# One row of steps for both batches' attention, with the first values behind two scores and the last values ahead of their sums

## The chip, the cores and the metric

The kernel runs on one core of a Trainium2 chip. The metric is the device time of one launch in microseconds (us), as a median over several executions. The engines are called as the profile calls them: PE is TensorE (PEld its weight loads), DVE VectorE, ACT ScalarE, POOL GpSimd, SP SyncE, which issues most DMAs.

## What is computed

Two layers on an input `x` of 2 batches x 256 channels x 56 x 56 pixels (3136 tokens a batch), all in fp32. The first is a linear non-local block (three 1x1 convolutions in 8 groups, no softmax), with a residual and a relu. The second is causal attention with 4 heads of 64, and then a mixture of 8 experts with the two best per token. Cut to what matters here:

```
x = relu(conv_block(x) + x)                          # layer 0
t = tokens(x)                                        # (2, 3136, 256)
q, k, v = heads(layernorm(t) @ W_attn)               # 4 heads of 64
att = softmax(where(causal, q @ k.T / 8, -big))
t = t + (att @ v) @ W_proj
g = layernorm(t);  probs = softmax(g @ gate_w + gate_b)
top2_vals, top2_idx = top_k(probs, 2)                # gate values are not renormalised
t = t + sum over the two experts e: w_e * (gelu(g @ W1[e] + b1[e]) @ W2[e] + b2[e])
```

## The kernel before

Names: `b` is the batch (B = 2), `hp` the pair of heads (NH = 2), `i` a block of 448 queries (NB = 7, W = 448), `j` a chunk of 128 keys (NCH = 25, the last has 64). Scores are held with keys on the partitions and two heads x 448 queries along the free axis, 896 elements.

**First layer** (0 to some 80 us): Gram matrices of `x`, folded into one matrix per batch, which is applied to `x`. The tokens `ts[b]` stay on chip and are also written to DRAM as `kept`.

**Attention, the fast path** (80 to some 850 us, batch 0 and then batch 1). For every (b, i, hp) the chunks that the causal mask admits are gone through. A *step* is one chunk: `scores` makes the products (L745, 8 PE instructions), exps without subtracting a maximum (ACT, L753), masks (DVE, L755, only on a chunk that the diagonal cuts) and adds the exps into an accumulator `acc` (DVE: the first chunk is copied, L763, the others added, L767). `values` multiplies the same exps with the values (L785) into a PSUM bank `yp`. Values run LAG = 3 steps behind the scores. When the last values of a (b, i, hp) are done, ACT copies `yp` into the tile that `acc` holds (L796) and POOL adds the two halves into `qT`, over the queries that are no longer needed (L797):

```
both = accs.pop((hp, i))
nc.scalar.copy(both, yp[:, :, :W])
nc.gpsimd.tensor_tensor(yh, both[:, 0], both[:, 1], ALU.add)
```

`sum_rows` makes the denominators: products of `acc` with ones (L809), an ACT copy (L814), and two DMAs by way of DRAM into row r = (b * 2 + hp) * 7 + i of a tile `sums`. The tasks in `later` follow some steps afterwards: `invert` (reciprocal, DMA out, two DMAs back, spread over the partitions), `scale` (L841) and `hand_on`, which tells by `finished` that these queries may be projected.

In every iteration n of the loop over steps, the order that all five engines keep is written out by hand: BEHIND = 2 steps after a (b, i, hp) has issued its last scores come `visit` (projections of the next block's queries, keys and values, L600 to L638) and its `sum_rows`; then `between` (pulls a piece of other work from a queue: projecting back, gate, dispatch, loads), due tasks, scores of step n, values of step n - 3. Where the values are the first of a (b, i, hp), the scores come ahead of them. Every batch has a row of steps and a call of `attend` of its own.

**Experts** (some 850 us to the end): tokens are sorted by expert into blocks of 128 slots. Rows are scattered to DRAM by indirect DMA on POOL (L1420), loaded block by block (102 blocks in the main loop, MAIN), transposed (L1518), multiplied (L1541, gelu on ACT at L1550, L1560) and gathered or added back into tokens (`finish`, gathers at L1738). `meanwhile` pulls queued work once a block; batch 1's scattering lies beside the first blocks.

**The second path.** `judge` looks, after batch 1's denominators, at the least and greatest element of `sums` on each partition; the number of partitions on which both lie in the bounds is kept in `good`, and in another element of it multiplied with whether the blocks were enough:

```
nc.vector.tensor_scalar(tiles[:, 2:3], tiles[:, 0:1], MOST, None, ALU.is_le)    # MOST = 1e25
nc.vector.tensor_scalar(tiles[:, 3:4], tiles[:, 1:2], LEAST, None, ALU.is_ge)   # LEAST = 1e-25
```

At the end of the program stands

```
with tc.If(n_done < P):
    n_good = count(0)
    with tc.If(n_good < P):
        ...                    # reads kept[b] back, statistics of every row
        layer1("g", True)
    late()
```

`layer1("g", True)` is the whole second layer once more, with names that end in `_g`: `attend_general` subtracts the true maximum of every query before the exps. It takes one head and 112 queries at a time, keeps the scores of all chunks in SBUF, has one PSUM bank for scores, one for values, and leaves the order of engines to the scheduler. `late()` is for blocks beyond the main loop and writes the whole output again.

Of the kernel before, what the change touches and what calls it, by code (L numbers as in the profile page):

```python
# [28 lines left out]
def conv_attn_moe_kernel(  # L29
# [482 lines left out]
    def layer1(nm, general):  # L512

        with ExitStack() as whole:
# [192 lines left out]

            def attend(
                b, qT, kT, v, fst, fs, psc, py, visit, between, clock, later, finished
            ):  # L710

                steps, firsts = [], {}
                for i in range(NB):
                    nk = -(-((i + 1) * W) // P)
                    whole_js = [j for j in range(nk) if (j + 1) * P - 1 <= i * W]
                    cut = [j for j in range(nk) if j not in whole_js]

                    order = whole_js[: max(0, len(whole_js) - len(cut))]  # L720
                    rest = whole_js[len(order) :]
                    if not order and rest:
                        order.append(rest.pop(0))
                    while cut or rest:
                        if cut:
                            order.append(cut.pop(0))
                        if rest:
                            order.append(rest.pop(0))
                    for hp in range(NH):
                        for r, j in enumerate(order):  # L730
                            steps.append((i, hp, j, r == 0, r == len(order) - 1, order))
                sts, accs, yps = {}, {}, {}

                def scores(n):
                    i, hp, j, first, last, order = steps[n]
# [25 lines left out]
                    if first:  # L761
                        acc = fs.tile([P, 2, W], F32, tag="acc", name=f"acc_{sn}")
                        nc.vector.tensor_copy(acc, st)  # L763
                        accs[hp, i] = acc
                    else:
                        acc = accs[hp, i]
                        nc.vector.tensor_tensor(  # L767
                            acc[:k, :, c0:], acc[:k, :, c0:], st[:k, :, c0:], ALU.add
                        )
                    sts[n] = st  # L770

                def values(n):
                    i, hp, j, first, last, order = steps[n]
# [4 lines left out]
                    if first:  # L778
                        yps[hp, i] = py.tile([P, 2, 512], F32, tag="y", name=f"yp_{sn}")
                    yp = yps[hp, i]  # L780
# [11 lines left out]
                    if last:  # L792

                        yh = qT[:, hp, i * W : (i + 1) * W]
                        both = accs.pop((hp, i))
                        nc.scalar.copy(both, yp[:, :, :W])  # L796
                        nc.gpsimd.tensor_tensor(yh, both[:, 0], both[:, 1], ALU.add)  # L797
                        del yps[hp, i]

                def sum_rows(hp, i):  # L800
# [3 lines left out]
                    acc = accs[hp, i]  # L804
# [18 lines left out]
                    later.append((clock[0] + 4, invert, hp, i, yh))  # L823

                def invert(hp, i, yh):
# [12 lines left out]
                    later.append((clock[0] + 6, lambda hp, i, yh: scale(hp, i, yh, rb), hp, i, yh))  # L838

                def scale(hp, i, yh, rb):  # L840
                    nc.vector.tensor_tensor(yh, yh, rb, ALU.mult)  # L841
                    later.append((clock[0] + 2, hand_on, hp, i, yh))

                def hand_on(hp, i, yh):
                    finished[hp] = (i + 1) * W

                def due(now):
                    while later and (now is None or later[0][0] <= now):
                        _, task, hp, i, yh = later.pop(0)
                        task(hp, i, yh)  # L850
                        later.sort(key=lambda e: e[0])

                ends = {i: max(n for n, s in enumerate(steps) if s[0] == i) for i in range(NB)}
                LAG, BEHIND = 3, 2
                for n in range(len(steps) + LAG):
                    if BEHIND < n <= len(steps) + BEHIND and steps[n - 1 - BEHIND][4]:
                        i, hp = steps[n - 1 - BEHIND][:2]
                        visit(i, hp)
                        sum_rows(hp, i)
                    if n < len(steps):  # L860
                        i = steps[n][0]
                        between(i, ends[i] - n, (steps[n][2] + 1) * P > i * W + 1)

                    late = n >= LAG and steps[n - LAG][3]
# [7 lines left out]
                    if late:  # L872
                        values(n - LAG)
                return due
# [561 lines left out]
            def experts(w1s, w2s, b2s, ex, es, ps6, between, need, written, settle, decide):  # L1436
# [63 lines left out]
                def experts_of(r):  # L1500

                    b = 0 if (r + 1) * GB <= FULL0 else 1
                    s = r * GB - known[b][0]
                    return nc.values_load_multi_w_load_instructions(
                        eblks[b][0:1, s : s + GB],
                        engines=(PE, DVE),
                        min_val=0,
                        max_val=E - 1,
                        skip_runtime_bounds_check_because="a count of at most E parts, cut to E - 1",
                    )[1]  # L1510

                def inputs(n, group):
                    xb, to = group
                    g = n % GB
# [165 lines left out]
                for n in range(-1, MAIN + 1):  # L1680
# [4 lines left out]
                    if n < 0:  # L1685
                        ids.extend(experts_of(0))
# [5 lines left out]
                    for m in (n + 1, n + 2):  # L1692
                        if m < MAIN and m not in wb:
                            wb[m] = weights(m)
                    if n == MAIN - 1:
                        decide()
# [21 lines left out]

            def finish(b, oy, bufs):
# [3 lines left out]
                def fetch(n, m, k):  # L1723
# [9 lines left out]
                    for c, y in enumerate(ys):  # L1733
                        for a in range(m):
                            while gathered[0] == 1 + turn[0] % 2:
                                yield False
# [61 lines left out]
                ahead, added = deque(), None  # L1798
                parts = deque(pairs())
                if b:  # L1800
                    parts = deque([(0, 1, P), *pairs(1, LAST)])
                while b == 0 and (parts or ahead):
                    if parts:
                        yield from fetch(*parts.popleft())
                    if len(ahead) == bufs or not parts:
# [184 lines left out]
            else:  # L1990
# [9 lines left out]
                def ahead(b, i, hp):  # L2000

                    xs, qks, vs = projections[b]
                    if i + 1 < NS:
                        if hp == 0:
                            return qks(i + 1), xs(i + 2)[:1]
                        return vs(i + 1), xs(i + 2)[1:]
# [3 lines left out]
                    if hp == 0:  # L2010
                        return [], xs(0)
                    return qks(0) + vs(0), xs(1)
# [20 lines left out]
                for piece in keys[2:] + vs(0) + xs(1):  # L2033
                    piece()
                for b in range(B):
                    batches.append(tokens(b, qT, lambda b=b: min(finished[b])))
# [4 lines left out]
                    def visit(i, hp):  # L2041

                        now, then = ahead(b, i, hp)
                        if b + 1 == B and i + 1 == NB and hp + 1 == NH:
                            nc.scalar.activation(warm, eps5[:1], AF.Gelu)
                        ring.append(0)
                        for piece in now:
                            piece()
                        for _ in range(2):
                            products()  # L2050
                        for piece in then:
                            piece()
                        ring.clear()

                    def between(i, left, cut):
                        if b == B - 1 and i == NB - 1 and left < NH * NCH - 2:

                            now = load_w2(left < NCH - 4)
                            for _ in range(1 if left > NCH - 4 else 2):
                                next(now, None)  # L2060

                        tick[0] += 1
                        if not cut or i:
                            pull()

                    due = attend(
                        b, qT, kT, v, fst, fs, psc, py, visit, between,
                        clock, later, finished[b],
                    )
# [20 lines left out]
            with ExitStack() as moe:  # L2090
# [23 lines left out]
                def written():  # L2114
# [4 lines left out]
                    for a in range(GB):  # L2119
                        hots.append(hot.tile([P, REST], F32, name=f"hot{a}_{nm}"))  # L2120
                        nc.gpsimd.iota(
                            hots[a], pattern=[[1, REST]], base=LAST * P - OFF, channel_multiplier=0,
                            allow_small_or_imprecise_dtypes=True,
                        )
# [3 lines left out]
                def meanwhile():  # L2128
                    gathered[0] = stored[0] = 0
                    turn[0] += 1  # L2130
                    if placed[1] and not sent[1]:
                        pull(2 + turn[0] % 2, every=True)
# [4 lines left out]
                    if side and next(side[0], None) is None:  # L2137
                        side.popleft()

# [10 lines left out]
                with tc.manual_schedule(engines={PE, DVE, POOL, SP, ACT}):  # L2150
                    experts(
                        first[0], w2s, b2s, ex, es, ps6,
                        meanwhile, need, written, settle, decide,
# [173 lines left out]
```

## Time and profile before

| | us |
|---|---|
| median of 3 runs (1262.29 to 1263.56) | 1262.87 |
| profiled execution | 1279.51 |
| its span | 1277.8 |
| PE busy in the span | 1251.2 |
| DVE / ACT / POOL busy | 786.6 / 613.2 / 357.9 |
| first layer, window 0 to 80: PE busy | 76.67 |
| attention of batch 0, window 80 to 464: PE busy | 381.63 |
| attention of batch 1, window 464 to 852: PE busy | 382.81 |
| experts, window 852 to 1277.8: PE busy | 410.08 |

The profiled execution is one of its own and 16.6 us longer than the median; durations and waits are read from it. The mean granted PE clock in it is 0.998. A row of the groups reads: line, engine, operation, output<-inputs, shape, count | busy us in total, mean ns of one | idle us of that engine just before, and what ended it. The ends of matmuls are modelled, so that a row's mean on PE times its count overstates the time in which PE works; the windows and the page count overlaps once. Lines are those of the kernel that the row belongs to.

### The profile page before, as it was taken

Reading aid. Unit: us, or ns where it says so; the run is one execution under the profiler, and the core shown is the slowest. Engines: PE = TensorE matmul, PEld = TensorE weight load, DVE = VectorE, ACT = ScalarE, POOL = GpSimd, SP = SyncE. Lnnn points to the kernel's source line nnn. Section 1 sums busy time; section 2 is a strip of 40 time slices with the busy share of each in tenths; the row PEclk is TensorE's granted clock in tenths of the full one; section 3 lists DMA queues with packets and bytes.
Section 4 is the critical chain, followed back from the end, with each engine's and each line's share of the span. In section 5 each row is a group of like instructions: output and inputs, shape, how many; then the busy total and the mean of one; then the engine's idle time right before and its main releaser. Section 6 shows DMA issues by size and latency. Waiting matters only on the chain.

```text
span 1277.8 us, 28550 instructions
## 1 busy us (share of the span) xinstructions
PE 1251.2 (98%) x10809; PEld 816.4 (64%) x10809; DVE 786.6 (62%) x1711; ACT 613.2 (48%) x1237; POOL 357.9 (28%) x319
## 2 busy tenths in 40 slices
PE   8999999999999999999999999999999999999998
PEld 8875545444444444545544443469889899899996
DVE  2673567666777745576677878785744443455664
ACT  0255555565556555455555655553333333344432
POOL 1103230000002204221102666100256112666651
PEclk9999999999999999999999999999999999999999
DMA  9995001000000000100000123541334333466654
GB/s 312 357 346 177 24 18 32 25 9 25 9 17 10 25 1 17 35 16 9 9 9 22 66 71 100 199 137 65 100 130 150 105 113 101 142 198 199 212 160 126
DMA packets 111073, 123.87 MB, mean 97 GB/s; under 512 B 19703, under 2 KB 100840, under 8 KB 110930
## 3 DMA queue, kind: packets, MB, share of 16 engines
q1 hardware_dynamic: 100274, 95.41, 24.2%
q0 software_dynamic: 9840, 25.67, 6.0%
q8 instruction: 89, 1.46, 0.5%
q10 hardware_dynamic: 816, 0.88, 0.2%
q14 instruction: 54, 0.44, 0.1%
HBM read 62.06 MB, written 61.05 MB: 96 GB/s over the span
## 4 chain that ended last, share of the span: by engine, by line
PE 93%; DVE 3%; issue 1%; ACT 1%; another core or an unknown queue 0%; DVEq 0%; DMA 0%; ACTq 0%
PE yp_f L785 20%; PE sc_f L745 20%; PE ht_f L1541 14%; PE yp_f L1560 13%; PE qk_f L614 7%; PE v_f L629 4%; PE pp_f L683 3%; PE cp L410 3%; PE gram L317 2%; PE tp_f L1518 2%; DVE acc_f L767 1%; PE sp_f L809 1%; PE yo_f L1787 1%; PE xp_f L600 1%; ACT st_f L753 1%
## 5 line engine op out<-in xcount | busy, mean ns | idle before, releaser
L767 DVE TENSOR_TENSOR acc_f<-acc_f,st_f 128x896 f32<-128x896 f32 (+5 forms) x372 | 373.1, 1003 | 127.2 <-ACT st_f L753 117.4
L753 ACT ACTIVATE st_f<-sc_f 128x896 f32<-128x896 f32 (+5 forms) x400 | 330.4, 838 | 203.2 <-PE sc_f L745 182.8
L785 PE MATMUL yp_f<-st_f,v_f 64*64 64x448 f32 (+6 forms) x3184 | 337.3, 500 | 3.8 <-DVE st_f L755 2.0
L745 PE MATMUL sc_f<-qT_f,kT_f 64*64 64x448 f32 (+6 forms) x3184 | 335.9, 499 | 1.5 <-ACT st_f L753 1.4
L1550 ACT ACTIVATE g_f<-ht_f,b1b 128x128 f32<-128x128 f32 x408 | 116.6, 372 | 234.0 <-PE ht_f L1541 116.0
L745 PEld LDWEIGHTS sc_f<-qT_f,kT_f 64*64 64x64 f32 x3184 | 118.9, 133 | 154.6 <-issue 139.2
L785 PEld LDWEIGHTS yp_f<-st_f,v_f 64*64 64x64 f32 x3184 | 116.5, 133 | 156.7 <-issue 126.7
L1541 PE MATMUL ht_f<-xT_f,w_f 128*128 128x128 f32 x1632 | 203.2, 276 | 7.4 <-issue 6.3
L1541 PEld LDWEIGHTS ht_f<-xT_f,w_f 128*128 128x128 f32 x1632 | 197.5, 192 | 14.4 <-issue 9.1
L1420 POOL DMA_INDIRECT x_slots<-xr_f,idx x100 | 120.5, 1205 | 146.6 <-DMA y_slots<-ys_f 62.9
L797 POOL TENSOR_TENSOR qT_f<-acc_f 128x448 f32<-128x448 f32 x28 | 32.0, 1143 | 450.1 <-ACT acc_f L796 450.1
L1529 DVE COPY w_f<-w1s_f 128x1024 f32 x102 | 72.4, 711 | 95.5 <-PE ht_f L1541 32.1
L585 POOL TENSOR_SCALAR xn_f<-t 128x256 f32<-128x256 f32 (+1 forms) x50 | 84.8, 1704 | 156.9 <-PE xp_f L600 68.6
L1581 POOL DMA_INDIRECT y_tokens<-ys_f,to_f x57 | 58.9, 1034 | 127.8 <-DVE ys_f L1570 107.7
L614 PE MATMUL qk_f<-px_f,wat 128*128 128x512 f32 (+2 forms) x224 | 88.2, 546 | 0.6 <-ACT px_f L606 0.6
L1570 DVE TENSOR_TENSOR ys_f<-yp_f,kT_f 128x128 f32<-128x128 f32 x102 | 29.5, 289 | 88.3 <-PE yp_f L1560 62.5
L614 PEld LDWEIGHTS qk_f<-px_f,wat 128*128 128x128 f32 x224 | 40.6, 190 | 45.7 <-issue 41.0
L1560 PE MATMUL yp_f<-px_f,g_f 128*128 x204 | 61.6, 383 | 1.3 <-issue 1.3
L1560 PE MATMUL yp_f<-kT_f,g_f 128*128 x204 | 61.1, 381 | 0.0
L1560 PE MATMUL yp_f<-v_f,g_f 128*128 x204 | 61.0, 381 | 0.0
L755 DVE TENSOR_TENSOR st_f<-st_f,keep 128x256 f32<-128x256 f32 (+1 forms) x112 | 44.9, 401 | 26.2 <-ACT st_f L753 25.6
L1560 PE MATMUL yp_f<-w2s_f,g_f 128*128 x204 | 60.7, 379 | 0.0
(287 smaller groups left out, 1224.8 us busy)
## 6 DMA issues: line engine op xcount, KB each, us to landing
x_slots<-fill SPq DMA_DIRECT2D x1, 8190.0 KB
xb_f<-x_slots SPq DMA_DIRECT2D x60, 130.0 KB
x_slots<-fill SPq DMA_DIRECT2D x1, 7296.0 KB
y_slots<-ys_f SPq DMA_DIRECT2D x57, 128.0 KB
kept<-t SPq DMA_DIRECT2D x2, 3200.0 KB
x<-in_x_dram SPq DMA_DIRECT2D x14, 448.0 KB
rb_f<-inverses SPq DMA_DIRECT2D x56, 112.0 KB
y_f<-y_tokens SPq DMA_DIRECT2D x23, 256.0 KB
```

The lines of the kernel that those rows point to most:

```text
L585: nc.gpsimd.tensor_scalar(xn[:k, a], ts[b][:k, n + a, :C], ts[b][:k, n + a, MEAN : MEAN + 1], ts[b][:k, n + a, RSTD : RSTD + 1], ALU.subtr ...
L614: nc.tensor.matmul(ps[:, :w], wat[:, c, d0 : d0 + P], px[:, s % 2, c, :w], start=(c == 0), stop=(c == NH - 1),)
L745: nc.tensor.matmul(ps[h : h + HS, a, c0:W], kT[hp][rows, j * P + h : j * P + h + HS], qT[rows, hp, q0 + c0 : q0 + W], start=True, stop=True,)
L753: nc.scalar.activation(st[:k, :, c0:], ps[:k, :, c0:W], AF.Exp, scale=SCALE)
L767: nc.vector.tensor_tensor(acc[:k, :, c0:], acc[:k, :, c0:], st[:k, :, c0:], ALU.add)
L785: nc.tensor.matmul(yp[a * HS : (a + 1) * HS, h // HS, c0:W], v[hp][h : h + HS, j, a, :HS], st[h : h + HS, a, c0:], start=first, stop=bool( ...
L1420: s = nc.gpsimd.indirect_dma_start(out=xds[b], out_offset=bass.IndirectOffsetOnAxis(ap=idxs[b][:kk, k, n : n + 1], axis=0), in_=xr[:kk], i ...
L1529: nc.vector.tensor_copy(w, w1s[:, :, bass.ds(e, 1), :].rearrange("p c e h -> p c (e h)"))
L1541: nc.tensor.matmul(ht[:, k, :], w[:, c, k * P : (k + 1) * P], xT[:, c, :], start=(c == 0), stop=(c == NH - 1),)
L1550: nc.scalar.activation(g[:, k, :], ht[:, k, :], AF.Gelu, bias=b1bs[b][:, k, i : i + 1])
L1560: nc.tensor.matmul(yp[:, :C], g[:, k, :], w2s[k][:, bass.ds(e, 1), :].rearrange("p e d -> p (e d)"), start=(k == 0), stop=(k == KH - 1),)
L1581: s = nc.gpsimd.indirect_dma_start(out=y_tokens, out_offset=bass.IndirectOffsetOnAxis(ap=to[:, n % GB : n % GB + 1], axis=0), in_=ys, in_o ...
```

## The change

- *One row of steps.* `attend` is called once; its steps are those of both batches, and everything it keeps is indexed by (b, hp, i). `open_batch` puts a batch's follow-up work into the queue when its first step comes. The projection of batch 1's first tokens begins two visits earlier; that of its first keys and values moves to the visit of batch 0's last block with hp = 0, which is put FREED + LAG = 7 steps behind instead of 2.
- *First values behind two scores.* Batch 0's first values `vs(0)` and the tokens after them are projected in a new visit ahead of step n = 2, where they stood ahead of the attention.
- *Last values ahead of the sums.* The final visit comes one step earlier, the cut chunks of the last block swap places with whole ones so that the 64-key chunk comes last, two inputs of the experts stage are transposed there (`early_input`, into `qT`), the ids of its first experts are read earlier, and the `sum_rows` of the final (b, i, hp) is called behind the loop.
- *No copy into `acc`.* The first chunk's exps stay in their tile until the second chunk; one add makes `acc`.
- *Experts stage.* While batch 1 scatters, `meanwhile` pulls one piece less and `amid`, in the middle of a block, pulls one; `finish` begins its gathers later; the three IOTAs (L2121) move into the gather loop of batch 0.

```
         if first:
-            acc = fs.tile([P, 2, W], F32, tag="acc", name=f"acc_{sn}")
-            nc.vector.tensor_copy(acc, st)
-            accs[hp, i] = acc
+            single[b, hp, i] = st
+        elif (b, hp, i) in single:
+            one = single.pop((b, hp, i))
+            acc = accs[b, hp, i] = fs.tile([P, 2, W], F32, tag="acc", ...)
+            nc.vector.tensor_tensor(acc[:, :, c0:], one[:, :, c0:], st[:, :, c0:], ALU.add)
+            if c0:
+                nc.vector.tensor_copy(acc[:, :, :c0], one[:, :, :c0])
...
         if last:
             yh = qT[:, hp, i * W : (i + 1) * W]
-            both = accs.pop((hp, i))
+            both = accs[b, hp, i]
             nc.scalar.copy(both, yp[:, :, :W])
             nc.gpsimd.tensor_tensor(yh, both[:, 0], both[:, 1], ALU.add)
...
+    LAG, BEHIND, FREED = 3, 2, 4
+    visits = {BEHIND: (0, -1, NH - 1)}
+    for n, s in enumerate(steps):
+        if s[5]:
+            change = s[0] + 1 < B and s[1:3] == (NB - 1, 0)
+            visits[n + 1 + (FREED + LAG if change else BEHIND)] = s[:3]
+    final = visits.pop(len(steps) + BEHIND)
+    visits[len(steps) + 1] = final
     for n in range(len(steps) + LAG):
-        if BEHIND < n <= len(steps) + BEHIND and steps[n - 1 - BEHIND][4]:
-            i, hp = steps[n - 1 - BEHIND][:2]
-            visit(i, hp)
-            sum_rows(hp, i)
+        if n in visits:
+            visit(*visits[n])
+            b, i, hp = visits[n]
+            if i >= 0 and visits[n] != final:
+                sum_rows(b, hp, i)
...
+    sum_rows(final[0], final[2], final[1])
     return due
...
     def ahead(b, i, hp):
+        if i < 0:
+            return vs(0), xs(1)
...
-        if hp == 0:
-            return [], xs(0)
-        return qks(0) + vs(0), xs(1)
+        if hp == 0:
+            return qks(0) + vs(0), xs(1)[:1]
+        return [], xs(1)[1:]
...
     def visit(b, i, hp):
+        if last and hp == 0:
+            early_ids.extend(experts_of(0))
+        if last and hp + 1 == NH:
+            nc.scalar.activation(warm, eps5[:1], AF.Gelu)
+            while len(early_rows) < 2:
+                pull(every=True)
+            now = [partial(early_input, n, qT) for n in range(2)]
...
-    while gathered[0] == 1 + turn[0] % 2:
+    while gathered[0] == (1 if turn[0] < since + 4 else 2 - (turn[0] % 4 == 0)) or turn[0] < since + 2:
...
     def meanwhile():
-            pull(2 + turn[0] % 2, every=True)
+            pull(1 + turn[0] % 2, every=True)
+    def amid():
+        if placed[1] and not sent[1]:
+            pull(every=True)
```

## The prediction

> **What bounds the kernel now.** I read the page first (busy time, then the chain), then the list of what TensorE waited for, the groups by shape, and the windows by stage. Page and chain:
>
> ```profile
> PE 1251.2 (98%) x10809; PEld 816.4 (64%) x10809; DVE 786.6 (62%) x1711; ACT 613.2 (48%) x1237; POOL 357.9 (28%) x319
> ...
> PE 93%; DVE 3%; issue 1%; ACT 1%; another core or an unknown queue 0%; DVEq 0%; DMA 0%; ACTq 0%
> ```
>
> TensorE (PE) is busy for 1251.2 of the 1277.8 us of the span and carries 93% of the chain. It is idle for 26.6 us in all, so an edit that removes no PE work can win no more than that. The list of PE's waits says where some of it lies (line waited at, releaser, total us, times, longest):
>
> ```profile
> PE ht_f L1541 <- issue: 6.3, 12, 1.0
> PE gram L317 <- DMA xr<-in_x_rows_dram: 3.1, 1, 3.1
> PE yp_f L785 <- DVE st_f L755: 2.0, 5, 0.8
> PE yp_f L785 <- ACT acc_f L796: 1.8, 3, 0.6
> ...
> PE sc_f L745 <- ACT st_f L753: 1.4, 3, 0.6
> ```
>
> The attention's waits (L745, L785) come to 5.2 us. Where they lie, the chain between 458 and 482 us tells (start, us, piece), where batch 0 ends and batch 1 begins:
>
> ```profile
> 475.42 0.59 ACT px_f L606
> 476.01 0.04 issue
> 476.06 0.59 PE sp_f L809 x8
> 476.64 0.96 PE yp_f L785 x8
> 477.60 0.03 ACTq L796
> 477.63 0.04 issue
> 477.67 0.72 ACT acc_f L796
> ```
>
> The sums of batch 0's last query block (L809) and its last values (L785) have no scores of batch 1 to run between.
>
> [...]
>
> **The change part by part.** Prices, from the groups by shape (us in total, mean ns of one):
>
> ```profile
> L763 DVE COPY acc_f<-st_f 128x896 f32<-128x896 f32 x28 | 18.0, 642 | 5.8 <-ACT st_f L753 5.5
> L767 DVE TENSOR_TENSOR acc_f<-acc_f,st_f 128x896 f32<-128x896 f32 x288 | 320.3, 1112 | 124.4 <-ACT st_f L753 117.4 <-DVE acc_f L767 0.4 <-issue 0.2
> L767 DVE TENSOR_TENSOR acc_f<-acc_f,st_f 128x128 f32<-128x128 f32 x12 | 3.6, 297 | 0.4
> L2121 POOL IOTA hot_f<- 128x448 f32 x3 | 1.9, 694 | 0.0
> ```
>
> *A. One row of steps, scores of batch 1 ahead of the last values of batch 0.* No instruction goes; 24 (8 sums, 16 value products) get company. Saves the boundary's idle: 20 - 19.16 and 20 - 19.12 in the windows 460:480 and 480:500, 1.7 us. The projections of batch 1's first keys and values move seven steps back in PE's row. PE work is the same; SP's DMAs for the sums keep their count.
>
> *B. First values behind two scores.* In the windows 80:100 and 100:120 PE is idle 0.6 and 1.3 us; up to 1.9 us go. The projected values (ACT copies L638) are then due later, and two exps are ahead of them on ACT: some of it comes back as a wait at L785.
>
> *C. The end of attention.* Two input transposes of the experts stage and two copies (L1522, 392 ns) come ahead of the last values. PE is busy 4.98 of the 6 us in 846:852, so at most 1.0 us goes. It brings a new wait: PE's transposes stand behind the DMA of two gathered row tiles, and the values of the last two steps are queued behind them. No view of before shows that wait; nothing (the rows already lie there) to 3 us, I take 0.5.
>
> *D. No copy into acc.* 28 x 642 ns = 18.0 us of DVE go; the first sum takes two exp tiles. DVE is 62% busy and PE waits for L767 only 0.3 us (at L809), so nothing on the path.
>
> *E. Experts stage.* One more pull in the middle of a block while rows are scattered, gathers begun two to four turns later, 3 x 694 ns of IOTA into a later loop. POOL is 28% busy; its order of DMA issues decides when the tail of the kernel gets its rows. PE's idle in 852:1278 is 426 - 410.08 = 15.9 us, of which the last 17.8 us hold 5.9. Between -3 (gathers land late) and +4 us; I take +1.
>
> Sum of A to E: 1.7 + 1.5 + 0.5 + 0 + 1 = **some 5 us** less, bounds -3 to 10.
>
> *F. The last sums after the last values.* This is where I expect the time to be decided. `values` on the last key chunk of a query block does `nc.scalar.copy(both, yp)` with `both = accs[...]`: it writes the finished values over the accumulator of exps, which is free by then because `sum_rows` has been issued before it. For 27 of 28 (batch, head pair, query block) this order stays. For the final one the change skips the visit's `sum_rows` and calls it behind the loop, after `values(last)`. In the order of instructions of the changed kernel the ones-products of these sums wait for the very ACT copy that overwrites the accumulator, on the same tile. So row 27 of `sums` holds, for each query, the sum over 64 + 64 partitions of unnormalised values rather than of exps. Evaluated from the reference's inputs, these 896 sums run from -11037.6 to 3951.1 and 836 of them are not positive; the right ones are all above 3000.
>
> `judge` compares each partition's least sum with LEAST = 1e-25 and its greatest with 1e25, and counts partitions that pass. With 836 of 896 below the bound, nearly all of the 64 that hold sums fail, `n_done < P` and `n_good < P` hold, and the kernel takes `tc.If`: it reads the tokens back from `kept`, runs `layer1("g", True)`, which is attention by `attend_general` and the whole experts stage again, and then `late()`. The output stays right; the page of before has no line of that path. So **the fallback comes on top of a whole run**.
>
> Its price by hand, from the order of the instructions. `attend_general` treats 112 queries of one head at a time: 2 batches x 4 heads x 28 = 224 units with 2936 key chunks, 13.1 a unit. On PE, a score product of 128x112 and a value product of 65x112 cost about what a 128x128 product does. L1541's 16 instructions (8 products) take about 2.0 us, so 0.25 a product; I use 0.24 and 0.22: 2936 x 0.46 = 1350 us; 896 spreads (0.2), 896 transposes (0.2): 360 us. Sum 1,710. [...] PE and DVE alternate, for the scores have one PSUM bank: product pair 0.48, three value products of the unit before 0.66, hand-overs 0.1, or 1.2 us for two chunks while ACT copies (L814: 128x224, 345 ns). 13.1 x 0.6 = 7.9 us, and 2.1 us a unit for maximum, transposes, spread and the first exps: **10 us x 224 = 2,240 us**. Lower bound 1,700 (busiest engine, no gap), upper 2,900 (13 us, nothing overlapped between units).
>
> ```profile
> 852.00:1278.00 426.00, 410.08 (x2794) 378.21 (x2792) 218.48 (x673) 157.82 (x536) 168.06 (x160) 0.99 0.45 139
> ```
>
> This window (its end is the end of the span) is the experts stage of before, 426 us with PE busy 410; run again, 430 us. The rest: branch and reading back 3.3 MB per batch 10 + 20; statistics 50 x 0.6 (L177, L178) = 30; projections of both batches 2 x 76 us of PE (88.2 at L614, 46.5 at L629, 14.3 at L600, in 2 batches) plus waits 200; projecting back and scattering after each attention (50 scatters at 1205 ns) 100; `late()` with 6 blocks at twice the 4.1 us that 426 us over 105 blocks gives, and 26 output steps of 3 us (four adds L1773 at 0.48, a copy L1792 of 0.59, hand-overs), 130. In all 2,240 + 430 + 30 + 30 + 200 + 100 + 130 = 3,160; some of the statistics and projecting back lies beside attention, so I take **3,100 us**.
>
> Against the profiled execution: 1279.5 - 5 + 3100 = 4375. That execution lies 16.6 us (1.3%) above the median of 1262.87; on the median, 1262.9 - 5 + 3100 = 4358. I say **4,350**.
>
> **The rivals.**
>
> *Fallback at another price.* Engines fully overlapped: attention 1,700, so 3,800 in all. Units strictly in series, [...] a slower granted clock: 2,900, so 5,020. For the first speaks that the scheduler mixes units on PE; for the second, the one score bank.
>
> *No fallback, and the edits pay (the other side).* If the last sums pass the bounds after all (the order I read isn't what runs, or the values there are positive), F costs nothing and A to E decide: 1262.9 - 5 = **1258**. It is one mechanism at one place: the comparison in `judge` with the sums of row 27. It decides at the first partition with a sum below 1e-25. Against it: 836 negative sums of 896.
>
> *No fallback, and the new waits cost.* The early transposes wait for row tiles in C, 3 us, or gathers come late in E, 3 us at the tail: 1266 to 1268. [...] against it, that POOL has idle time 72% of the span.
>
> **How the numbers follow.** A measurement of this kernel tells some 0.2%, 2.5 us, from no change. Fallback 0.94 (all slower by far); no fallback 0.06: faster 0.035, within 0.2% 0.015, slower 0.01. Predicted: 4350. The range reaches from 3,700 (just below full overlap) to 5,050 (just above series); it leaves out the fast cases (6%) and about one in eight within the fallback.
>
> **What would show it.** Right: the span is three to four times as long; a second set of names ending in `_g`; the DVE maxima of 128x112 as the costliest group of DVE, near 300 ns; ones-products of row 27 behind the ACT copy; between the end of the first pass and the first `_g` product a gap of some tens of us with no PE work. In the first part, A to D: no 128x896 DVE copies, the boundary without its 1.7 us. Wrong: a span near 1270 us with no `_g` names; then F fell at `judge`.

## The result, and the profile after

The changed kernel takes **5521.66 us** (median of 6, 5512.22 to 5545.64) against 1262.71 us before: a ratio of 4.374 [4.368, 4.379]. It computes the second layer twice. Direction and path were as predicted; the time lies above the range of 3700 to 5050 us.

The page after: totals, the row of PE's granted clock (40 slices of 138 us, in tenths of full speed), and the chain by engine and line.

```profile
PE 5124.2 (93%) x28988; PEld 3905.4 (71%) x28988; DVE 2550.9 (46%) x7793; ACT 1707.8 (31%) x4363; POOL 688.6 (12%) x818
...
PEclk9999999998555556555555865655555565569995
...
PE 90%; DVE 3%; ACT 3%; issue 2%; DMA 2%; POOL 0%; SPq 0%; DVEq 0%; ACTq 0%; POOLq 0%
PE gsc L935 28%; PE gyp L1007 21%; PE yp_f L788 5%; PE sc_f L744 5%; PE ht_f L1570 3%; PE ht_g L1570 3%; PE yp_g L1589 3%; PE yp_f L1589 3%; PE mb L914 3%; PE gyrb L914 2%; PE gtp L974 2%; PE pp_g L683 2%; ACT gst L948 2%; PE qk_f L614 2%; PE qk_g L614 1%
```

The chain leads with L935 and L1007, the score and value products of `attend_general` (14 lines further down than in the kernel before), and with names in `_g`. PE is busy for 93% of the span, a figure that looks like before's 98%; the clock row tells the difference: 9 while the first pass runs, 5 to 6 in most of the general attention, 9 again in the experts stage.

The windows by stage (us, then PE, PEld, DVE, ACT, POOL busy with counts, granted clock, DMA share, GB/s):

```profile
1252.00:1300.00 48.00, 3.49 (x18) 2.85 (x17) 22.88 (x106) 2.86 (x6) 4.30 (x7) 0.51 1.08 360
1300.00:1384.00 84.00, 78.73 (x273) 46.76 (x274) 4.55 (x25) 34.62 (x94) 31.90 (x29) 0.95 0.26 79
1384.00:4943.00 3559.00, 3336.62 (x14884) 2619.65 (x14883) 1510.45 (x5261) 878.39 (x2445) 118.71 (x297) 0.57 0.02 6
4943.00:5360.00 417.00, 404.75 (x2797) 377.11 (x2797) 211.29 (x642) 161.29 (x539) 168.68 (x160) 0.99 0.45 141
5360.00:5518.00 158.00, 57.29 (x206) 42.21 (x206) 26.40 (x74) 16.39 (x43) 5.84 (x6) 0.59 0.35 106
```

Reading back and statistics 48 us, projection of batch 0 84, both general attentions with batch 1's projection between them 3559, the experts stage again 417, `late` 158: together 4266 us. That is the whole rise (5521.7 - 1262.7 = 4259).

PE's waits in the whole trace:

```profile
PE gsc L935 <- ACT gst L948: 103.5, 271, 0.4
PE yo L2293 <- DVE y L2288: 64.7, 13, 7.1
PE wg_g L565 <- ACT wT_g L557: 44.2, 1, 44.2
...
PE yp_f L788 <- ACT acc_f L799: 1.8, 3, 0.6
...
PE yp_f L788 <- DVE st_f L754: 1.1, 2, 0.8
PE sp_f L812 <- ACT acc_f L799: 1.1, 1, 1.1
```

The last line is the step that the prediction rested on: the final sums wait for the ACT copy over their accumulator. The timeline between 833 and 856 us has the four instructions in that order (start, us, engine, line):

```profile
843.15 1.08 PE L788 MATMUL yp_f<-st_f,v_f 64*64 64x448 f32 x12
...
844.33 0.91 ACT L799 COPY acc_f<-yp_f 128x896 f32<-128x896 f32 x1 [0.54 <-PE yp_f L788]
845.28 0.59 PE L812 MATMUL sp_f<-acc_f,ones 128*32 128x224 f32 x8 [1.05 <-ACT acc_f L799]
845.31 1.26 POOL L800 TENSOR_TENSOR qT_f<-acc_f 128x448 f32<-128x448 f32 x1 [33.96 <-ACT acc_f L799]
```

The sums (L812) and the addition of the two value halves (L800) start off the same tile within 0.03 us of each other: what is summed are values.

### The profile page after: what moved, and what is told of

The parts are those of the page before. It is cut to its first block, busy times and chain, and to the rows that moved or that the text cites. A ratio compares the mean times of both kernels' runs of the same rounds, so it can differ in the third digit from the quotient of the medians.

```text
span 5518.0 us, 79625 instructions
## 1 busy us (share of the span) xinstructions
PE 5124.2 (93%) x28988; PEld 3905.4 (71%) x28988; DVE 2550.9 (46%) x7793; ACT 1707.8 (31%) x4363; POOL 688.6 (12%) x818
## 4 chain that ended last, share of the span: by engine, by line
PE 90%; DVE 3%; ACT 3%; issue 2%; DMA 2%; POOL 0%; SPq 0%; DVEq 0%; ACTq 0%; POOLq 0%
PE gsc L935 28%; PE gyp L1007 21%; PE yp_f L788 5%; PE sc_f L744 5%; PE ht_f L1570 3%; PE ht_g L1570 3%; PE yp_g L1589 3%; PE yp_f L1589 3%; PE mb L914 3%; PE gyrb L914 2%; PE gtp L974 2%; PE pp_g L683 2%; ACT gst L948 2%; PE qk_f L614 2%; PE qk_g L614 1%
## 5 line engine op out<-in xcount | busy, mean ns | idle before, releaser
L935 PE MATMUL gsc<-qT_g,kT_g 64*128 64x112 f32 (+4 forms) x5872 | 1697.6, 426 | 133.2 <-ACT gst L948 103.5
L935 PEld LDWEIGHTS gsc<-qT_g,kT_g 64*128 64x128 f32 x5872 | 1278.1, 295 | 510.9 <-issue 215.3
L1007 PE MATMUL gyp<-gst,v_g 128*65 128x112 f32 (+4 forms) x5872 | 1193.9, 372 | 39.4 <-ACT gst L992 32.7
L952 DVE TENSOR_TENSOR rm<-rm,gst 128x112 f32<-128x112 f32 x2544 | 693.9, 273 | 1061.1 <-ACT gst L948 1001.6
L1007 PEld LDWEIGHTS gyp<-gst,v_g 128*65 128x65 f32 x5872 | 946.3, 209 | 192.9 <-issue 106.0
L948 ACT COPY gst<-gsc 128x224 f32<-128x224 f32 (+1 forms) x1328 | 448.0, 337 | 1989.8 <-PE gsc L935 1982.7
L770 DVE TENSOR_TENSOR acc_f<-acc_f,st_f 128x896 f32<-128x896 f32 (+6 forms) x344 | 344.7, 1002 | 120.6 <-ACT st_f L752 111.3
L752 ACT ACTIVATE st_f<-sc_f 128x896 f32<-128x896 f32 (+6 forms) x400 | 330.4, 838 | 201.5 <-PE sc_f L744 185.1
L989 DVE TENSOR_TENSOR gst<-gst,mb 128x896 f32<-128x896 f32 (+7 forms) x408 | 341.5, 877 | 110.0 <-PE mb L914 103.5
L992 ACT ACTIVATE gst<-gst 128x896 f32<-128x896 f32 (+7 forms) x408 | 307.9, 784 | 117.1 <-DVE gst L989 116.5
L788 PE MATMUL yp_f<-st_f,v_f 64*64 64x448 f32 (+6 forms) x3184 | 337.2, 500 | 3.0 <-ACT acc_f L799 1.8
L788 PEld LDWEIGHTS yp_f<-st_f,v_f 64*64 64x64 f32 x3184 | 117.6, 133 | 154.0 <-issue 129.0
```

The lines of the kernel that those rows point to most:

```text
L752: nc.scalar.activation(st[:k, :, c0:], ps[:k, :, c0:W], AF.Exp, scale=SCALE)
L770: nc.vector.tensor_tensor(acc[:k, :, c0:], acc[:k, :, c0:], st[:k, :, c0:], ALU.add)
L788: nc.tensor.matmul(yp[a * HS : (a + 1) * HS, h // HS, c0:W], v[hp][h : h + HS, j, a, :HS], st[h : h + HS, a, c0:], start=first, stop=bool( ...
L935: nc.tensor.matmul(dst[:k], kT[hp][r0 : r0 + HS, j * P : j * P + k], q[:, c0:], start=True, stop=True,)
L948: nc.scalar.copy(st[:, j0 : j0 + m, :].rearrange("p a q -> p (a q)"), ps[:, : m * QW])
L952: nc.vector.tensor_tensor(rm, rm, st[:, j0 + jj, :], ALU.max)
```

## The experiments

Each ratio is to runs of the kernel before on the same chip (medians 1276.1 to 1280.4 us there). Savings in us below are the ratio's distance from 1 on 1262.7 us.

**flaw** is before with the order of F alone.

```
-   sum_rows(hp, i)
+   if (b, i, hp) != (B - 1, NB - 1, NH - 1): sum_rows(hp, i)
...
+   if b == B - 1: sum_rows(NH - 1, NB - 1)        # behind the loop
```

> The kernel before with one edit: the sums of the final (b, hp, i) are issued behind the loop, after the ACT copy that overwrites their accumulator; nothing else of the change. Theory: the second path is taken, 1262.7 + 4260 = 5520 to 5530 us. Rival (the second path needs the rest of the change): 1263 us, with wrong sums only.

5544.6 us, ratio 4.336 [4.290, 4.382]. F alone is enough for the second path, at the same time within the interval.

**forced** is before with `LEAST = 1e9`.

> The kernel before with LEAST = 1e9 in place of 1e-25, so that right sums (above 3000) fail the bound. Theory (the time is that of the second path on top of a whole run, whatever the sums are): 5520 to 5530 us, as flaw. If wrong sums cost by themselves (tokens with odd routing), flaw is longer than this by more than 10 us.

5551.1 us, ratio 4.341 [4.306, 4.376]: the same as flaw. The time is that of running twice; wrong sums add nothing that two runs can show.

**fix** takes the overwriting of the final accumulator away from the changed kernel.

```
-   both = accs[b, hp, i]
+   both = accs[b, hp, i] if (b, i, hp) != (B - 1, NB - 1, NH - 1) else fst.tile([P, 2, W], F32, tag="st", ...)
```

> The changed kernel with one edit: for the final (b, hp, i) the ACT copy of the finished values goes into a tile of the exps' pool and not over the accumulator. Theory (the overwritten accumulator sends the kernel down the second path): no names ending in _g, and the edits A to E alone, 1262.7 - 5 = 1258 us (range 1253 to 1266). Rival (the second path is taken for another reason, such as a changed verdict): again some 5520 us.

5586.4 us, ratio 4.382 [4.368, 4.395]. **The rival's number.** The final sums are not the only thing that sends the kernel there.

**fix_noC** puts the whole end of attention back to the order before.

> As the changed kernel, with the end of attention as before: the final visit two steps behind, its sums inside the loop and so ahead of the copy that overwrites the accumulator, whole and cut chunks in the old order, no early inputs. The second path must not be taken under the theory: 0.5 us more than fix by the prediction (C gave 0.5), at most 1.0 more, and up to 3 less if the wait for the row tiles costs what its bound says. If the second path came from any other part of the change (A, B, D, E), this kernel takes it too: 5520 us.

5583.8 us, ratio 4.377 [4.372, 4.383]: the second path again, so its cause lies outside C as well. **fix_noE** (experts stage as before) and **fix_noD** (copy of the first exps put back) were run as well, each on fix:

> As fix, with the experts stage as before: pulls of 2 and 3 pieces between blocks, none in the middle, gathers as before, the three IOTAs in one place. If E is worth the 1 us that the prediction gave it, 1 us more than fix; if E is where the gain lies, 3 to 5 us more; if its late gathers cost, less than fix by up to 3 us.

> As fix, with the copy of the first exps into the accumulator put back (28 x 642 ns = 18 us of DVE). If DVE is off the path, as the prediction says, within 1 us of fix; if the copies delayed something, up to 4 us more.

5559.1 us (4.355 [4.344, 4.366]) and 5581.8 us (4.370 [4.359, 4.380]). With the second path in, they tell nothing of E and D; they do tell that neither part is needed to send the kernel there.

What is left is A or B, and in A there is a suspect. Its loop makes `sum_rows` part of a visit, and one visit, that of (0, 6, 0), was moved from BEHIND = 2 to FREED + LAG = 7. Counted from the block's last scores, its sums now come 8 steps later (3 before), and the copy of its values over the accumulator still comes 3 steps later. **fix2** is fix with these sums taken out of the late visit:

```
    visits[n + 1 + (FREED + LAG if change else BEHIND)] = s[:3]
+   if change: early = n + 1 + BEHIND, s[:3]
...
-   if i >= 0 and visits[n] != final:
+   if i >= 0 and visits[n] not in (final, early[1]):
        sum_rows(b, hp, i)
+   if n == early[0]:
+       b, i, hp = early[1]
+       sum_rows(b, hp, i)
```

> As fix (the final copy into a spare tile), and the sums of batch 0's last block with hp = 0 issued 2 steps behind its last scores again, ahead of its last values, while its projections stay 7 steps behind. New theory: a second accumulator was overwritten in the change, that of (0, 6, 0), whose sums moved back with its visit to 8 steps after its last scores while its values were copied over it 3 steps after; the prediction overlooked it. Then this kernel does not take the second path: 0.4% or 5 us less than before on the same chip, between 10 less and 3 more. Rival (something else in A or B fails the bounds): 4.38 times before again.

**1275.56 us, ratio 0.9955 [0.9940, 0.9970]**: no second path, and faster than before by 5.7 us [3.8, 7.6]. The timelines of ACT and PE between 418 and 456 us show the difference; first the changed kernel, then fix, then fix2:

```profile
425.92 0.90 ACT L799 COPY acc_f<-yp_f 128x896 f32<-128x896 f32 x1
...
447.05 0.58 PE L812 MATMUL sp_f<-acc_f,ones 128*32 128x224 f32 x8
```

```profile
426.51 0.90 ACT L799 COPY acc_f<-yp_f 128x896 f32<-128x896 f32 x1
...
447.64 0.58 PE L812 MATMUL sp_f<-acc_f,ones 128*32 128x224 f32 x8
```

```profile
425.42 0.58 PE L812 MATMUL sp_f<-acc_f,ones 128*32 128x224 f32 x8
...
427.03 0.91 ACT L799 COPY acc_f<-yp_f 128x896 f32<-128x896 f32 x1 [0.26 <-issue]
```

In the changed kernel and in fix the copy is 21 us ahead of the sums of its tile, in fix2 1.6 us behind them. The place of these sums is all in which the code of fix and fix2 differs. So the changed kernel overwrites two accumulators, and either alone sends it down the second path: the final one in flaw, that of (0, 6, 0) in fix.

**The parts A to E, on fix2.** noE, noC and noD are the edits named above; noB projects the first values ahead of the attention again; fix2_in issues the final sums in the final visit, ahead of the last values, with no spare tile.

> As fix2, with the experts stage as before. By the prediction 1 us more than fix2 (bounds 3 less to 4 more).

> As fix2, with the end of attention as before (final visit two steps behind with its sums in it, old order of the last chunks, no early inputs, no spare tile). By the prediction 0.5 us more than fix2 (bounds 3 less to 1 more).

> As fix2 with the copy of the first exps put back (18 us of DVE). By the prediction within 1 us of fix2, since DVE is off the path; if DVE was late somewhere, up to 4 us more.

> As fix2 with batch 0's first values projected ahead of the attention again. By the prediction 1.5 us more than fix2 (PE's idle time at the start of attention comes back), bounds 0 to 2.

> As fix2, but the final sums are issued in the final visit, ahead of the last values, so that no spare tile is needed. If the order of the last values and their sums is worth anything by itself, up to 0.8 us more than fix2; else the same within 0.2%.

| | ratio to before | us less than before |
|---|---|---|
| fix2 | 0.9955 [0.9940, 0.9970] | 5.7 [3.8, 7.6] |
| fix2_noE | 0.9971 [0.9958, 0.9985] | 3.7 [1.9, 5.3] |
| fix2_noC | 0.9971 [0.9961, 0.9980] | 3.7 [2.5, 4.9] |
| fix2_noD | 0.9971 [0.9963, 0.9979] | 3.7 [2.7, 4.7] |
| fix2_noB | 0.9979 [0.9969, 0.9989] | 2.7 [1.4, 3.9] |
| fix2_in | 0.9988 [0.9979, 0.9997] | 1.5 [0.4, 2.7] |

noE, noC and noD can't be told from fix2: their intervals overlap, and C, D and E may each be worth anything from nothing to some 4 us. noB just touches fix2's interval. Taken at face value, the four losses would add up to 9 us, more than the 5.7 of the whole, so part of them is scatter or interplay. No run takes A out. fix2_in is apart from fix2, by 4 us, where 0.8 at most was expected. The chains from 843 us of fix2_in and of fix2 show where:

```profile
843.77 0.62 ACT L2097
...
845.07 0.20 ACT warm L2097
845.27 0.26 ACT qT_f L1476
...
845.58 0.59 PE sp_f L812 x8
846.16 1.04 PE yp_f L788 x12
```

```profile
844.93 0.59 PE first_f L1473 x4
845.51 0.89 PE pp_f L683 x4
846.41 1.04 PE yp_f L788 x12
```

In fix2_in the chain goes through ACT: the table load for the gelu (0.62 us of it lie on the chain; the changed kernel's trace has it as 1.28 us of ACT_TABLE_LOAD at 841.77) and a copy of an early input (0.26) come ahead of the sums (L812), and these ahead of the last values. In fix2 the last values follow PE's other work without a wait. PE is busy 17.52 of the 20 us from 840 to 860 in the one and 19.72 in the other. fix2_noC, which also has the sums ahead of the last values, but no early inputs, stands between them with 19.00. So the place of the sums alone does not explain the 4 us; sums that stand behind the early inputs do, as far as these chains show. With the early inputs, the last values ahead of their sums is the better order; it needs a tile of its own for the result.

**The price of the second path.** Four kernels tell what the clock follows. **micro** has stretches of single shapes and leaves the layers out:

> No part of the reference: PE products of one shape after another on the same data, each stretch behind 120 products of 128x128x128 that bring the clock to full. Stretches: A scores' shape (64 rows, 128 columns, 112 moving) without waits; B values' shape (128 rows, 65 columns, 112 moving); C two of A and three of B in turn, without waits; D as C, with one bank and an ACT copy after each pair; F as A with 224 moving; G 128 rows, 128 columns, 112 moving; H as A with 448 moving; I as B with 448 moving; J pairs of A with the ACT copy alone; K 128x128 with 64 moving. If the shape sets the clock (part of the array, or share of the time in which columns stream), A, B and C run below 0.7 and G or H at 1.00: G at 1.00 with A low says that rows count, H and F at 1.00 say that the streaming share counts. If waits set it, A, B and C run at 1.00 and D and J fall.

The windows of its stretches A, B, C, D and J:

```profile
36.40:81.00 44.60, 44.60 (x400) 44.56 (x400) 0.00 (x0) 0.00 (x0) 0.00 (x0) 1.00 0.00 1
108.20:146.00 37.80, 37.80 (x397) 37.80 (x396) 0.00 (x0) 0.00 (x0) 0.00 (x0) 1.00 0.01 1
173.40:253.00 79.60, 79.60 (x592) 64.73 (x592) 0.00 (x0) 0.00 (x0) 0.00 (x0) 1.00 0.00 1
281.00:361.00 80.00, 79.93 (x595) 65.00 (x594) 0.00 (x0) 20.37 (x59) 0.00 (x0) 1.00 0.00 1
...
748.50:846.00 97.50, 68.53 (x238) 53.09 (x239) 0.00 (x0) 20.36 (x59) 0.00 (x0) 0.52 0.00 0
```

The shapes of the general attention run at 1.00 where nothing waits, and so does D, which was to fall if waits count: the value products there cover the ACT copy (PE is busy 79.93 of 80 us). J is the same score products with the copy uncovered: 0.52. In these stretches the low clock goes with the waits and not with the shape, though PE waits only 0.49 us at a time, as a cycle of J shows:

```profile
791.13 0.34 ACT L89 COPY res<-mixJ 128x224 f32<-128x224 f32 x1 [1.33 <-PE mixJ L87]
791.52 0.92 PEld L87 LDWEIGHTS mixJ<-xt 64*128 64x128 f32 x4 [0.76 <-ACT res L89]
791.53 1.19 PE L87 MATMUL mixJ<-xt 64*128 64x112 f32 x4 [0.49 <-ACT res L89]
```

**micro2** varies the number of products n to a copy:

> No part of the reference: chains on one PSUM bank, n products of 128x128x112 and then an ACT copy of 112 columns that the next n wait for, for n = 1, 2, 3, 4, 5, 6, 8, 10, 12, 16; 120 products without waits ahead of each. At full clock a product is 0.22 us, and the copy with its hand-overs some 0.5 us, so PE works for 0.3 of the time at n = 1, 0.47 at 2, 0.57 at 3, 0.64 at 4, 0.73 at 6, 0.88 at 16. If the granted clock follows the share of the time that PE works, there is an n below which it is 0.50 and above which it is 1.00, with no wait anywhere as long as 1 us. If only long idle stretches lower it, all run at 1.00 and stretch J of the earlier run was an exception.

Windows for n = 2, 3, 4 and 5:

```profile
140.00:198.00 58.00, 43.67 (x147) 34.03 (x148) 0.00 (x0) 9.11 (x36) 0.00 (x0) 0.50 0.00 0
240.00:296.00 56.00, 44.85 (x167) 37.64 (x168) 0.00 (x0) 6.91 (x28) 0.00 (x0) 0.50 0.00 0
326.00:368.00 42.00, 31.26 (x219) 26.48 (x220) 0.00 (x0) 6.84 (x27) 0.00 (x0) 1.00 0.00 1
398.00:440.00 42.00, 32.17 (x237) 27.92 (x236) 0.00 (x0) 6.09 (x24) 0.00 (x0) 1.00 0.00 1
```

0.50 up to n = 3, 1.00 from n = 4 on (to 16): a step. PE is idle for 0.40 us in a cycle at n = 3 and at n = 4 alike; with the one product more the clock is full and not half. The busy share of the profile does not tell it: 44.85 of 56 us, 80%, at n = 3 and half clock, 31.26 of 42, 74%, at n = 4 and full clock. Every stretch of micro and micro2 begins behind 120 products of 128x128x128. Behind J the clock rises with them, from 0.53 between 845 and 852 us to 1.00 between 852 and 859. So these runs show where the clock falls, not which of the attention's shapes would bring it back.

**forced_sc2** and **forced_sc3** give the scores of the general attention two and three PSUM banks (`bufs=1` to 2; to 3, with the banks for maxima, spreads and sums going from 3 to 2).

> As forced, with two PSUM banks for the scores of the general attention. If the low granted clock (0.50 to 0.60 there) comes from PE's short waits for the one score bank, the clock rises above 0.9 and the time falls by 1000 us or more. If it comes from the shapes (half of the array's rows or columns, 112 moving columns per weight load), the clock stays below 0.7 and the time falls by at most the 123 us that PE waited for score banks (L935).

> As forced_sc2 with three banks for scores (and two in place of three for maxima, spreads and sums). Theory (waits of PE on ACT and DVE lower the clock, and the clock is what the prediction's price of 10 us a unit missed): the clock in the general attention rises above the 0.68 of two banks and the time falls below 4,705 us. If two banks already took all of it, within 1% of 4,705; if the banks taken from maxima and spreads make new waits, longer.

4704.6 us (ratio 3.679 [3.668, 3.690]) and 4390.3 us (3.434 [3.425, 3.442]). The general attentions in windows, of forced, forced_sc2 and forced_sc3:

```profile
1404.00:4984.00 3580.00, 3357.63 (x14882) 2637.21 (x14882) 1511.03 (x5261) 878.15 (x2444) 118.85 (x298) 0.56 0.02 6
```

```profile
1400.00:4120.00 2720.00, 2602.98 (x14886) 2209.72 (x14886) 1463.04 (x5264) 865.49 (x2447) 119.68 (x298) 0.68 0.03 8
```

```profile
1410.00:3790.00 2380.00, 2259.07 (x14815) 1955.13 (x14815) 1436.69 (x5248) 848.64 (x2438) 119.07 (x295) 0.76 0.03 9
```

The same work takes 3580, 2720 and 2380 us at clocks of 0.56, 0.68 and 0.76. In the changed kernel's list PE waits 123 us in all for score banks (L935, 103.5 of them for ACT's copy); the second bank was worth 846 us (5551.1 against 4704.6). What the waits don't explain fits the clock: time times clock is some 2,000, 1,850 and 1,810 us, an estimate from these three windows, so that at full clock the three would lie within some 10%. Neither forecast was right: for waits the clock was to rise above 0.9; for shapes it was to stay below 0.7, which 0.68 does, but the gain was to be 123 us at most. With three banks PE still waits 67.0 us for exps (L993 on ACT L978); whether these waits hold the clock down there was not shown, for no run takes them away.

## Why the prediction was right or wrong

*F, the overwritten sums.* Right in what it does: flaw shows it alone, the timeline from 843 us shows it in the changed kernel. Wrong in one sentence: "For 27 of 28 this order stays". It stays for 26; the late visit takes (0, 6, 0) along. I had read the seven steps for the projections that move with the visit and not for the sums that move with it. It cost the forecast nothing, since one bad row is enough, but a mend that follows the prediction fails, as fix did. One reading is wrong without effect: the row's 896 sums lie on all 128 partitions, 7 on each, and not on 64; one partition below the bound is enough.

*A to E, some 5 us, bounds -3 to 10.* Right in the sum: 5.7 [3.8, 7.6] in fix2. The parts did not come as given, so that is in part luck. PE's idle time, fix2 against before:

- A, 460 to 500 us: 1.26 against 1.72, so 0.5 where 1.7 was given. The one PSUM bank for `yp` is the wait that is left there (L788 on the ACT copy L799, 1.3 us in two waits between 410 and 520 us; before, 0.6 in one).
- B, 80 to 120 us: 1.23 against 1.92. But fix2_noB, without B, has 1.32 there, so B's own share is 0.1 of the 1.5 given.
- C, 840 to 860 us: 0.28 against 1.02, so 0.7 where 0.5 was given; fix2_noC is back at 1.00. No wait for the row tiles appeared.
- E, most of it in 860 to 1240 us: 9.91 against 9.78, nothing where 1 was given.

These windows make 1.8 us of the 5.7. The two profiled executions lie only 2.5 us apart (spans of 1275.3 and 1277.8), so the traces do not hold the rest, and the runs of the parts lie too close to each other to place it.

*The price of the second path, 3,100 us.* Too low by 1,160. The failing term is **10 us a unit, 2,240 us**, and in it the prices of 0.24 and 0.22 us a product, which are near those of a full clock: micro has 0.22 and 0.19 at 1.00 (two instructions a product: 400 in 44.60 us in A, 397 in 37.80 in B). With some 80 us of projecting between the batches (3116 to 3196) taken from 3559, a unit took 15.5 us (3,480 in all, projecting back within it included, for which the prediction had 100 apart). That is more than the 13 us of its upper bound. Two stretches of the same loop (part of the chain) show both clocks; first from 2121 us, in a window of 5 us with a clock of 0.96, then from 2143 us, in one with 0.50:

```profile
2121.87 0.72 PE gyp L1007 x6
2122.59 0.62 PE gsc L935 x4
```

```profile
2143.13 1.31 PE gyp L1007 x6
2144.44 1.12 PE gsc L935 x4
```

1.34 us for two chunks, near the 1.2 that I took, and 2.43. At half clock PE is busy without a gap in such a stretch (5.00 of 5.00 us from 2140), so that the one score bank hardly shows among the waits, though forced_sc2 shows what it is worth.

So the price failed on the clock and not on the order of the work: 3559 us at 0.57 is some 2,030 us at full clock, an estimate, against 2,240. The prediction named "a slower granted clock" within its series rival but gave it no price of its own, and that rival's 5,020 was too low as well: it bounded the time by gaps (1,700 to 2,900) as if PE's speed were given.

The other terms held: experts 417 (430), `late` 158 (130), start 48 and 84 against 60 and 100. DVE's costliest group, the running maxima, was 2544 x 273 ns (named: near 300); the branch cost PE no time that can be seen: its first product of the second path is at 1251.57, after 0.68 us of idle time that the last copy of the first path ends (ACT L1829). The 10 us for it, an estimate by choice, were too many. PE then stood 44.2 us for the reading back and the statistics.

*The rivals.* "No fallback, and the edits pay" was wrong for the changed kernel; its 1258, 5 less than before, is what fix2 shows (5.7 less) once both accumulators are kept. The waits that the third rival feared did not cost in fix2.

## What to carry to other kernels

When a task is moved in a hand-written order, list every tile that it reads and who writes it next: with every wait in place, a later read of the same tile reads something else. A kernel with a guarded slow path turns such an error into time, since that path computes everything again: its names in the profile are the first thing to look for. And before pricing PE's work in a loop that has not run, ask what PE waits for in it: a busy share of 93% hid the loss here, and the row of the granted clock showed it (5 to 6 tenths).

## What was not expected of the hardware

Two chains in which PE was idle for less than half a microsecond at a time ran at half clock: three products of 128x128x112 to a copy, with 0.40 us of idle time in a cycle, at 0.50, and J, with 0.49 us, at 0.50 in the windows of 7 us from 754 to 845 us. Four products to a copy, with the same 0.40 us, ran at 1.00.

Once at half clock, PE in the general attention was busy without a gap for 15 us (5.00 of 5.00 us in each window of 5 us from 2135 to 2150) and stayed at 0.50; after another such stretch (5.00 of 5.00 us from 2115) it was at 0.96. What the clock follows, and why it sometimes took long to rise, these runs leave open: a fourth product between pauses of the same 0.40 us lengthens the work and raises its share, reckoned at one clock, and no run parts the two.
